# A selective scan in four engines: one state of four scanned in PSUM, its inputs spread by matmuls, its sums kept channels first

## The chip, the cores and the metric

One core of a Trainium2 chip runs the whole program. The metric is device time in microseconds for one execution. A core has five engines with an instruction stream each: TensorE (PE in the profile, with PEld for its weight loads), VectorE (DVE), ScalarE (ACT), GpSimd (POOL) and SyncE (SP). In this program every DMA is issued by SP, in one order. PSUM is the small memory that PE writes; here it is eight tiles of 128 partitions by 512 float32 numbers. POOL has no operand in PSUM in either kernel.

## The reference, cut to what matters

Four images of 64 x 64 tokens and 96 channels go through two state-space layers and then two attention and feed-forward layers (the last two are not touched). Both state-space layers have this core: an input projection and a 3 x 3 convolution give u; u is read in four directions k (rows, columns, and both backwards); for each direction and channel d, sixteen states n are run along the tokens:

```python
xs = [u, u_transposed, u_reversed, u_transposed_reversed]
delta = softplus(dts + bias)
def step(h, inputs):                     # over all tokens, one after the other
    dA = exp(delta[..., None] * A)       # A: one number per channel and state
    h = h * dA + (delta * u)[..., None] * B[:, :, None, :]
    y = einsum('bkdn,bkn->bkd', h, C)    # sum over the 16 states
    return h, y
ys = ys + D * u
y = ys[0] + reversed(ys[2]) + transposed(ys[1]) + transposed(reversed(ys[3]))
y = layer_norm(y) * silu(z)              # z: the other half of the input projection
out = y @ out_proj.T
```

B and C depend on token and state, not on the channel. Layer 0 has 4 images of 4096 tokens and 192 channels. Layer 1 works on the 64 x 33 frequencies of a Fourier transform, so 2112 tokens, with 384 channels, and comes back by an inverse transform.

## The kernel before, in words

Channels lie on partitions, tokens along the free axis. In layer 0 two images share the 128 partitions (64 channels each, NI = 2), so 192 channels make C = 3 chunks; in layer 1 one image has 3 chunks of 128 channels (NI = 1). The work is a list of six phases, two for layer 0 (a pair of images each) and four for layer 1. A phase has four directions, a direction a row of segments: 8 of 512 tokens in layer 0, and 512, 512, 384, 384 and 320 in layer 1. That is 64 segments in layer 0 and 80 in layer 1. A segment has 12 steps: four quads q of four states, times three chunks c. So there are 768 steps in layer 0 (all of 512 tokens) and 960 in layer 1 (384 of 512, 384 of 384 and 192 of 320).

One step takes four states of one chunk:

- ACT makes four tensors of decays, exp(delta * A) (`exp`, L635). Two of them (`ax`) lie in SBUF, made a step ahead; two (`ay`) lie in PSUM.
- For states 0 and 1 (`hx`) the input b = delta * u * B comes from ACT and PE: `make_bx` (L600) multiplies the transposed delta * u, tokens on partitions, by B as a scale per partition, for all three chunks at once, and PE turns it back into a PSUM tile by transposes of 128 x 128 (`transposed`, L630).
- For states 2 and 3 (`hy`) B is loaded by a DMA that repeats its row on all partitions (`broadcast`, L580) and POOL multiplies (`front_b`, L653).
- DVE runs the four recurrences, one `tensor_tensor_scan` each (`scan`, L660), in token order or against it.
- The two pairs are multiplied by C, which comes repeated on all partitions too: `hx` on POOL (L805), `hy` on DVE (L822). The last column of each pair is kept as the state for the next segment (`keep_state`, L673, on POOL or ACT).
- PE adds the products up over the 16 states in a PSUM tile per chunk, by transposes of 128 x 128 that accumulate (`accumulate`, L682): 16 a step at 512 tokens, with the result tokens first. After the last quad ACT takes the sum out (`close_chunk`, L709) and it is stored tokens first, each direction apart.

PSUM's eight tiles are three accumulators (`acc0` to `acc2`), three in a ring for b and `ay` (`ab`), one for preparing the next segment (`pp`) and one for the side work (`ms`).

The order of all engines but SP is written out by hand in the loop over steps, and the engines hold to it. Between the parts of a step stand three slots; a slot takes a piece of the preparation of the next segment (`prepare`: projections to B, C and delta on PE, softplus on ACT in a `burst`, delta * u on DVE, transposes) and, at a rate per phase (`RATES`), a piece of side work. The side work is what the other phases need: input projection and convolution (L176, L274), transposing u (`flip`), z (`gate`), the end of a layer (`gated`) with `out0` or `out1`, the Fourier transforms and the attention layers (`tokens`). `gated` reads the four stored directions back tokens first (`load`), adds D * u (L397, a matmul with a diagonal) and the four directions (L403, transposes) in PSUM, 128 tokens at a time, and goes on with the norm, the gate and the output projection. Side work that PE meets in its order holds up the scan if it has to wait. A head of some 216 us precedes the first scan, and a tail of 390 us follows the last (the end of the last image, run four tasks wide).

Of the kernel before, what the change touches and what calls it, by code (L numbers as in the profile page):

```python
# [29 lines left out]
class Cfg:  # L30
# [5 lines left out]
    def __init__(self, pre, NI, KI, NR, nat, R, parts, rows, segs, eps):  # L36
# [8 lines left out]
        self.eps = eps  # L45


CFG0 = Cfg("l0", 2, 1, HH, 0, 6, [(0, 32), (32, 64)], [8] * 8, [512] * 8, 1e-5)
CFG1 = Cfg("l1", 1, 2, WF, 1, 12, [(0, WF)], [8, 8, 6, 6, 5], [512, 512, 384, 384, 320], 1e-5)
# [74 lines left out]
class Block:  # L124
# [79 lines left out]
    def in_weights(self, sp, g, c, w):  # L204
        cfg = self.cfg
        wi = sp.tile([CH, cfg.KI, 2, cfg.PI], F32, name=f"{cfg.pre}_wi_{g}_{c}", tag=f"wi{w}", bufs=2)
        self.nc.sync.dma_start(out=wi, in_=self.w["inw"][:, :, :, c, :])
        return wi

    def project(self, E, g, io):  # L210
# [8 lines left out]
        def chunk(sp, c, w):  # L219
# [4 lines left out]
            wi = self.in_weights(sp, g, c, w)  # L224
# [127 lines left out]
    def gated(self, E, g, io, out_proj):  # L352
# [5 lines left out]
        yn, yo = io["y"][cfg.nat], io["y"][1 - cfg.nat].rearrange("k (w r) c -> r w k c", r=cfg.NR)  # L358
        u, gz = io["u"][cfg.nat], io["gz"]
        with E.pool(f"{cfg.pre}nm{g}") as sp:  # L360
            wo = sp.tile([P, C, self.w["wo"].shape[2]], F32, name=f"{cfg.pre}_wo_{g}", tag="wo")
            nc.sync.dma_start(out=wo, in_=self.w["wo"])

            def load(b, i, r, n):
                nm = f"{cfg.pre}_{g}_{r}"
                yt = sp.tile([P, 2, 2, C * P], F32, name=f"yt_{nm}", tag=f"yt{b % W}", bufs=2)
                nc.sync.dma_start(
                    out=yt[: n * 64, 0], in_=yn[:, r * 64 : (r + n) * 64, :].rearrange("k t c -> t k c")
                )
                for m in range(n):  # L370
                    nc.sync.dma_start(out=yt[m * 64 : (m + 1) * 64, 1], in_=yo[r + m])
                ut = sp.tile([P, C, P], F32, name=f"ut_{nm}", tag=f"ut{b % W}", bufs=2)
                nc.sync.dma_start(out=ut[:, :, : n * 64], in_=u[:, :, r * 64 : (r + n) * 64])
                return yt, ut

            def worker(w):

                blocks = list(enumerate(cfg.rows))[w::W]
                todo = iter([(b, i, r + i, min(2, n - i)) for b, (r, n) in blocks for i in range(0, n, 2)])
# [4 lines left out]
                for b, (r, nr) in blocks:  # L384
# [5 lines left out]
                    for i in range(0, nr, 2):  # L390
                        m = min(2, nr - i) * 64
                        yt, ut = nxt
                        more = next(todo, None)
                        nxt = load(*more) if more else None
                        ps = E.psum(f"py_{nm}_{i}")[:, : C * P].rearrange("p (c t) -> p c t", c=C)
                        for c in range(C):
                            nc.tensor.matmul(  # L397
                                ps[:, c, :m], self.skip[:, c, :], ut[:, c, :m], start=(c == 0), stop=False
                            )
                        yield  # L400
                        for c in range(C):
                            for k in range(4):
                                nc.tensor.matmul(  # L403
                                    ps[:, c, :m],
                                    yt[:m, k // 2, k % 2, c * P : (c + 1) * P],
                                    self.ident[:m, :m],
                                    start=False,
                                    stop=(c == C - 1 and k == 3),
                                    is_transpose=True,
                                )  # L410
                            if c < C - 1:
                                yield
# [67 lines left out]
def scans(tc, ctx, phases, ident):  # L480
# [239 lines left out]
    with tc.manual_schedule(engines=IN_ORDER):  # L720
# [42 lines left out]
        for i, st in enumerate(steps):  # L763
# [26 lines left out]
            if nxt:  # L790
                nxt.ay = {}
                front_x(nxt)
# [704 lines left out]
```

## Time and profile before

| | |
|---|---|
| median of 3 runs | 11720.34 us (11690.25 to 11727.8) |
| profiled execution, its span | 11704.4 us, 16 us under that median |
| instructions in the trace | 164864 |
| busy share of the span: PE, PEld, DVE, ACT, POOL | 79%, 57%, 90%, 78%, 76% |
| mean granted TensorE clock | 0.880 |
| DMA | 1270879 packets, 1469.07 MB, engines 45.5% busy |

In the rows below, a row names line, engine, operation, what it writes and reads, shape, count, and then the summed time and the mean of one. PE's records overlap, so a busy PE is not a full one: for PE the time from one start to the next is what counts, and it is read from long runs of equal records without a gap. A float32 matmul shows as two records (two passes over its columns); a float32 transpose shows as one. The stages of the kernel are, in microseconds from the span's start: head 0 to 216, the two phases of layer 0 to 2767 and 5353, the four of layer 1 to 6823, 8270, 9791 and 11309, then the tail.

### The profile page before, as it was taken

Reading aid. Unit: us, or ns where it says so; the run is one execution under the profiler, and the core shown is the slowest. Engines: PE = TensorE matmul, PEld = TensorE weight load, DVE = VectorE, ACT = ScalarE, POOL = GpSimd, SP = SyncE. Lnnn points to the kernel's source line nnn. Section 1 sums busy time; section 2 is a strip of 40 time slices with the busy share of each in tenths; the row PEclk is TensorE's granted clock in tenths of the full one; section 3 lists DMA queues with packets and bytes.
Section 4 is the critical chain, followed back from the end, with each engine's and each line's share of the span. In section 5 each row is a group of like instructions: output and inputs, shape, how many; then the busy total and the mean of one; then the engine's idle time right before and its main releaser. Section 6 shows DMA issues by size and latency. Waiting matters only on the chain. (4 is left out here: it accounts for less than half of the span.)

```text
span 11704.4 us, 164864 instructions
## 1 busy us (share of the span) xinstructions
PE 9301.7 (79%) x54800; PEld 6722.3 (57%) x54800; DVE 10549.4 (90%) x10183; ACT 9089.0 (78%) x18533; POOL 8931.5 (76%) x7075
## 2 busy tenths in 40 slices
PE   6678888787888878877888888888778877788765
PEld 3455555555666556555665565565556655565554
DVE  6899999999999998999888989988999999899974
ACT  3778888898888888887767878877787787777753
POOL 2889999887887897897768878877767767677640
PEclk8789999988988998998889989988879988898887
DMA  5454454555555445445544353454225432443242
GB/s 145 120 142 119 126 127 115 141 155 158 153 153 129 124 124 141 120 127 162 153 129 124 114 147 120 142 150 119 88 79 158 122 96 92 124 137 106 83 117 42
DMA packets 1270879, 1469.07 MB, mean 126 GB/s; under 512 B 496071, under 2 KB 1033871, under 8 KB 1260679
## 3 DMA queue, kind: packets, MB, share of 16 engines
q1 hardware_dynamic: 1270023, 1458.53, 45.5%
q8 instruction: 430, 7.05, 0.3%
q14 instruction: 426, 3.49, 0.1%
HBM read 1221.74 MB, written 236.50 MB: 125 GB/s over the span
## 5 line engine op out<-in xcount | busy, mean ns | idle before, releaser
L653 POOL TENSOR_TENSOR hy_l<-du_l,bc_l 128x512 f32<-128x512 f32 (+2 forms) x3456 | 3957.3, 1166 | 1934.8 <-DVE hcy_l L822 960.1
L805 POOL TENSOR_TENSOR hcx_l<-hx_l,bc_l 128x1024 f32<-128x1024 f32 (+2 forms) x1617 | 3525.5, 2180 | 239.1 <-DVE hx_l L660 197.9
L600 ACT ACTIVATE bx_l<-dut_l,bt_l 128x192 f32<-128x192 f32 (+2 forms) x6272 | 2793.7, 498 | 0.0
L682 PE MATMUL acc_l<-ident,hcx_l 128*128 128x128 f32 (+1 forms) x12006 | 1876.0, 305 | 392.6 <-POOL hcx_l L805 388.4
L635 ACT ACTIVATE ax_l<-delta_l,l_alog 128x512 f32<-128x512 f32 (+2 forms) x3456 | 2139.1, 667 | 0.0
L682 PE MATMUL acc_l<-ident,hcy_l 128*128 128x128 f32 (+1 forms) x12000 | 1841.9, 302 | 302.4 <-DVE hcy_l L822 299.0
L682 PEld LDWEIGHTS acc_l<-ident,hcy_l 128*128 128x128 f32 (+1 forms) x12000 | 1551.5, 155 | 859.2 <-DVE hcy_l L822 475.7
L682 PEld LDWEIGHTS acc_l<-ident,hcx_l 128*128 128x128 f32 (+1 forms) x12006 | 1526.4, 156 | 861.5 <-POOL hcx_l L805 665.9
L822 DVE TENSOR_TENSOR hcy_l<-hy_l,bc_l 128x1024 f32<-128x1024 f32 (+2 forms) x1616 | 1951.1, 1207 | 43.6
L660 DVE TENSOR_TENSOR_SCAN hx_l<-ax_l,state_l,b_l 128x512 f32<-128x512 f32 (+2 forms) x1650 | 1787.4, 1124 | 212.7 <-PE b_l L630 136.9
L660 DVE TENSOR_TENSOR_SCAN hy_l<-b_l,state_l,hy_l 128x512 f32<-128x512 f32 (+2 forms) x1649 | 1782.9, 1118 | 89.3 <-ACT b_l L635 81.4
L635 ACT ACTIVATE b_l<-delta_l,l_alog 128x512 f32<-128x512 f32 (+2 forms) x1913 | 1196.6, 628 | 627.6 <-DVE hx_l L660 599.0
L630 PE MATMUL b_l<-ident,bx_l 128*128 128x128 f32 (+1 forms) x6724 | 1169.6, 302 | 363.0 <-DVE hy_l L660 203.5
L635 ACT ACTIVATE ab_l<-delta_l,l_alog 128x512 f32<-128x512 f32 x1321 | 907.1, 689 | 547.5 <-DVE hx_l L660 496.4
L630 PEld LDWEIGHTS b_l<-ident,bx_l 128*128 128x128 f32 (+1 forms) x6724 | 827.1, 152 | 861.3 <-DVE hy_l L660 337.1
L660 DVE TENSOR_TENSOR_SCAN hy_l<-ab_l,state_l,hy_l 128x512 f32<-128x512 f32 x961 | 1172.1, 1257 | 60.8 <-POOL hy_l L653 31.9
L660 DVE TENSOR_TENSOR_SCAN hx_l<-ax_l,state_l,ab_l 128x512 f32<-128x512 f32 x962 | 1176.5, 1263 | 49.3 <-PE ab_l L630 27.3
L630 PE MATMUL ab_l<-ident,bx_l 128*128 128x128 f32 x5288 | 889.1, 305 | 383.2 <-DVE hy_l L660 206.3
L673 POOL COPY state_l<-hx_l 128x2 f32<-128x2 f32 x1344 | 1141.9, 850 | 0.0
L630 PEld LDWEIGHTS ab_l<-ident,bx_l 128*128 128x128 f32 x5288 | 652.0, 154 | 715.6 <-DVE hy_l L660 326.6
L274 PE MATMUL pc_l<-pad_l,l_dg 128*128 128x512 f32 (+2 forms) x1656 | 787.9, 564 | 56.0 <-ACT uh_l L252 46.6
L176 PE MATMUL pi_l<-xi_l,l_wi 96*128 96x384 f32 (+6 forms) x912 | 458.6, 619 | 180.0 <-ACT zh_l L342 60.4
(225 smaller groups left out, 11821.3 us busy)
## 6 DMA issues: line engine op xcount, KB each, us to landing
bc_l<-l_xd_l SPq DMA_DIRECT2D x1536, 256.0 KB
bc_l<-l_xd_l SPq DMA_DIRECT2D x384, 512.0 KB
bc_l<-l_xd_l SPq DMA_DIRECT2D x384, 384.0 KB
us_l<-l_u SPq DMA_DIRECT2D x96, 768.0 KB
l_y<-y_l SPq DMA_DIRECT2D x288, 256.0 KB
bc_l<-l_xd_l SPq DMA_DIRECT2D x192, 320.0 KB
yt_l<-l_y SPq DMA_DIRECT2D x264, 192.0 KB
yt_l<-l_y SPq DMA_DIRECT2D x128, 384.0 KB
```

What stands on the lines that cost most here:

```text
L176: self.nc.tensor.matmul(out[i * cfg.PI : (i + 1) * cfg.PI, :n], wi[:, ki, half, :], xin[:, max(i, ki), :n], start=(ki == 0), stop=(ki == c ...
L274: nc.tensor.matmul(pc[:, : n * 64].rearrange("p (r w) -> p r w", w=64), diag[:, t, :], pad[:, r - p0 + dy : r - p0 + dy + n, dx : dx + 64] ...
L600: nc.scalar.activation(t[:n, b, :, ch], z.dut[:n, b, :, ch], AF.Copy, scale=z.bt[:n, b, m : m + 1])
L630: nc.tensor.transpose(pb[:, t : t + n], st.z.bx[st.q, j][:n, b, st.c], ident[:n, :n])
L635: nc.scalar.activation(out, z.delta[:, st.c, : z.S], AF.Exp, scale=z.blk.A[:, st.c, z.k, n : n + 1])
L653: nc.gpsimd.tensor_tensor(st.hy[:, j, :S], st.z.du[:, st.c, :S], st.z.b[st.q][:, j, :S], ALU.mult)
L660: nc.vector.tensor_tensor_scan(h[:, j, : z.S][:, ::step], a[:, : z.S][:, ::step], b[:, : z.S][:, ::step], 0.0 if z.first else z.state[st.c ...
L673: copy(z.state[st.c][:, n0 : n0 + 2].rearrange("p (j o) -> p j o", o=1), h[:, :, e : e + 1])
L682: nc.tensor.matmul(z.acc[st.c][:n, b, :], hc[:, j, t : t + n], ident, start=(n0 + j == 0 and b == 0), stop=(n0 + j == NST - 1 and b == 0), ...
L805: nc.gpsimd.tensor_tensor(hcx[:, :, :S], hx[:, :, :S], z.c[q][0][:, :, :S], ALU.mult)
L822: nc.vector.tensor_tensor(hcy[:, :, :S], st.hy[:, :, :S], z.c[q][1][:, :, :S], ALU.mult)
```

## The change

Per step, the four states are now treated in this way:

- B-scaled identities in place of B-scaled inputs. ACT multiplies the identity by B as a scale per partition (`make_diagonals`, L606 of the new kernel), 128 x 128 for each block of tokens, image of the pair, and made state. PE multiplies the transposed delta * u by them (`spread_b`, L639), which gives b with channels first. This is done for `made` states: 2 of 4 in layer 0 and 3 of 4 in layer 1. In layer 0 each image of the pair has its own B, so each is a matmul with 64 output partitions. POOL's `front_b` (L665) makes the other 2 or 1.
- One state (`kept` = 1) is scanned in place in its PSUM tile (L676); DVE multiplies it there by C (`multiply_kept`, L694) and ACT saves its last column. The other three lie in one SBUF tile, and POOL multiplies them by C in one instruction (`multiply`, L705), a step later than their scans, and saves their last columns.
- The sum over states is a matmul with the identity as weights over all tokens of the segment (`add`, L713), one per state, with channels first; its result is stored channels first. To a backward direction the forward one of the same kind is added in that sum, and D * u to the first (`fetch_more`, L737).
- `gated` reads two arrays, channels first, in place of four; one lies transposed, and is loaded in runs of 16 or 17 tokens (`load_crossed`, L380). It adds them by two identity matmuls per chunk and up to 512 tokens.
- C is loaded for four states at a time, B for two or one, at the first and second step of a quad. Some buffers of side work lose their second copy. The `ab` ring stays at three tiles.

The order of a step changes with it. Before: scan 0, scan 1, POOL's product, scan 2, scan 3, sums of the first pair, DVE's product, POOL's inputs, sums of the second pair. Now: scan 0, DVE's product of it, POOL's product of the step before, POOL's inputs for the next, the sum of the kept state, scan 1, scan 2, the three sums of the step before, scan 3, with the spreading matmuls of the next step after scans 1, 2 and 3.

```diff
-CFG0 = Cfg("l0", 2, 1, HH, 0, 6, [(0, 32), (32, 64)], [8] * 8, [512] * 8, 1e-5)
-CFG1 = Cfg("l1", 1, 2, WF, 1, 12, [(0, WF)], [8, 8, 6, 6, 5], [512, 512, 384, 384, 320], 1e-5)
+CFG0 = Cfg("l0", 2, 1, HH, 0, 6, [(0, 32), (32, 64)], [8] * 8, [512] * 8, 1e-5, 2, 1)
+CFG1 = Cfg("l1", 1, 2, WF, 1, 12, [(0, WF)], [8, 8, 6, 6, 5], [512, 512, 384, 384, 320], 1e-5, 3, 1)
...
-                    nc.scalar.activation(
-                        t[:n, b, :, ch], z.dut[:n, b, :, ch], AF.Copy, scale=z.bt[:n, b, m : m + 1]
-                    )
+                    nc.scalar.activation(
+                        t[:n, b, i, j, :n], ident[:n, :n], AF.Copy, scale=z.bt[:n, b, m : m + 1]
+                    )
...
-            nc.tensor.transpose(pb[:, t : t + n], st.z.bx[st.q, j][:n, b, st.c], ident[:n, :n])
+            for i in range(z.cfg.NI):
+                ch = slice(i * PI, (i + 1) * PI)
+                nc.tensor.matmul(
+                    pb[ch, t : t + n], z.dut[:n, b, st.c, ch], z.dg[st.q][:n, b, i, j, :n], start=True, stop=True
+                )
...
+            nc.vector.tensor_tensor(hk[:, : z.S], st.px[j][:, : z.S], z.c[st.q][:, j, : z.S], ALU.mult)
...
+        nc.gpsimd.tensor_tensor(st.hc[:, :, :S], st.h[:, :, :S], z.c[st.q][:, kept:, :S], ALU.mult)
...
-                nc.tensor.matmul(
-                    z.acc[st.c][:n, b, :],
-                    hc[:, j, t : t + n],
-                    ident,
-                    start=(n0 + j == 0 and b == 0),
-                    stop=(n0 + j == NST - 1 and b == 0),
-                    is_transpose=True,
-                )
+    def add(st, w, v, first=False, final=False):
+        nc.tensor.matmul(st.z.acc[st.c][:, : st.z.S], w, v[:, : st.z.S], start=first, stop=final)
...
+            scan(st, 0)
+            for j in range(made, 3):
+                front_y(st, j)
             if nxt:
-                nxt.ay = {}
                 front_x(nxt)
+            multiply_kept(st)
+            front_y(st, 3)
+            if closing:
+                close_chunk(closing)
+            closing = None
             long = burst()
-            scan(st, hx, 1, st.ax[:, 1], st.px[1], 4 * q + 1)
+            if before:
+                multiply(before)
+            if nxt:
+                front_b(nxt)
+            add_kept(st)
...
             slot(None)
+            scan(st, 1)
...
+                spread_b(nxt, 0)
             more.take(skip=long)
-            scan(st, st.hy, 0, st.ay[0], st.hy[:, 0], 4 * q + 2)
+            scan(st, 2)
+            if before:
+                add_rest(before)
+                closing = before if before.q == NQ - 1 else None
+            slot(None, hold=long)
             if nxt:
-                nxt.px.append(transposed(nxt, 1))
-            slot(None, hold=long)
-            scan(st, st.hy, 1, st.ay[1], st.hy[:, 1], 4 * q + 3)
+                spread_b(nxt, 1)
+            scan(st, 3)
+            if nxt:
+                for j in range(2, nxt.z.cfg.made):
+                    spread_b(nxt, j)
```

## The prediction

> **What bounds the kernel now.** I read four views: the page's engine shares, busy time by stage, the timeline of a steady stretch, and long gapless runs on PE for the price of a matmul. First the page:
>
> ```profile
> PE 9301.7 (79%) x54800; PEld 6722.3 (57%) x54800; DVE 10549.4 (90%) x10183; ACT 9089.0 (78%) x18533; POOL 8931.5 (76%) x7075
> ...
> L653 POOL TENSOR_TENSOR hy_l<-du_l,bc_l 128x512 f32<-128x512 f32 (+2 forms) x3456 | 3957.3, 1166 | 1934.8 <-DVE hcy_l L822 960.1
> L805 POOL TENSOR_TENSOR hcx_l<-hx_l,bc_l 128x1024 f32<-128x1024 f32 (+2 forms) x1617 | 3525.5, 2180 | 239.1 <-DVE hx_l L660 197.9
> ```
>
> DVE is busiest. The six scan stages (stretch; then PE, PEld, DVE, ACT, POOL busy, the clock granted to PE, DMA share, GB/s) say the same everywhere:
>
> ```profile
> 216.00:2767.00 2551.00, 1966.03 (x10846) 1355.87 (x10844) 2419.42 (x1992) 2167.24 (x4485) 2264.40 (x1643) 0.89 0.50 130
> 2767.00:5353.00 2586.00, 2099.21 (x12844) 1592.02 (x12843) 2436.35 (x2041) 2179.46 (x4537) 2213.66 (x1598) 0.90 0.53 137
> 5353.00:6823.00 1470.00, 1251.74 (x7299) 917.10 (x7298) 1306.77 (x1310) 1105.06 (x2120) 1142.68 (x968) 0.88 0.48 138
> 6823.00:8270.00 1447.00, 1236.57 (x7383) 882.46 (x7382) 1295.60 (x1303) 1124.74 (x2186) 1146.69 (x975) 0.90 0.46 131
> 8270.00:9791.00 1521.00, 1200.79 (x7235) 873.21 (x7233) 1425.94 (x1576) 1176.99 (x2429) 1079.85 (x932) 0.86 0.36 107
> 9791.00:11309.00 1518.00, 1185.08 (x7259) 869.74 (x7258) 1411.42 (x1558) 1155.70 (x2376) 1076.84 (x932) 0.87 0.36 105
> ```
>
> DVE is busy 10,295 of 11,093 us in the scans, 92.8%. One step of layer 0 on DVE, from one `hx` pair to the next, has no gap over 0.1 us and takes 6.14 us:
>
> ```profile
> 3008.64 2.45 DVE L660 TENSOR_TENSOR_SCAN hx_l<-ax_l,state_l,b_l 128x512 f32<-128x512 f32 x2
> ...
> 3011.01 2.43 DVE L660 TENSOR_TENSOR_SCAN hy_l<-b_l,state_l,hy_l 128x512 f32<-128x512 f32 x2
> ...
> 3013.48 1.22 DVE L822 TENSOR_TENSOR hcy_l<-hy_l,bc_l 128x1024 f32<-128x1024 f32 x1
> ...
> 3014.78 2.45 DVE L660 TENSOR_TENSOR_SCAN hx_l<-ax_l,state_l,b_l 128x512 f32<-128x512 f32 x2
> ```
>
> So half of L822 would be the gain, if nothing else takes DVE's place. For PE, busy time overstates, so I price it by pitch, the time from start to start:
>
> ```profile
> 3021.16 1.04 PE L682 MATMUL acc_l<-ident,hcy_l 128*128 128x128 f32 x8
> ```
>
> ```profile
> 79.95 14.00 PE L274 MATMUL pc_l<-pad_l,l_dg 128*128 128x512 f32 x32
> 93.89 1.72 PE L176 MATMUL pi_l<-xi_l,l_wi 96*64 96x448 f32 x4
> ```
>
> ```profile
> 11417.24 1.61 PE L397 MATMUL py_l<-ut_l,l_skip 128*128 128x128 f32 x12
> 11418.68 1.58 PE L403 MATMUL py_l<-ident,yt_l 128*128 128x128 f32 x13
> ```
>
> ```profile
> 11494.68 20.16 PE L1026 MATMUL piv<-ih,at 128*64 128x64 f32 x320 [1.51 <-DMA at<-att]
> ```
>
> A transpose of 128 columns costs (1.04 - 0.27 for the last one's latency) / 7 = 0.11 us. A float32 matmul is two records: at 512 columns each is 13.94 / 32 = 0.435, so 0.87 a matmul; at 128 columns each is 1.44 / 12 = 0.12, so 0.24. L1026 alternates two halves of 64 outputs, as the new L639 does in layer 0: 20.16 / 320 = 0.063 a record, at 64 columns.
>
> PE's work now is 24 transposes a step at 512 tokens (8 of L630, 16 of L682) and 18 at 384 and 320. 1152 x 24 x 0.11 + 576 x 18 x 0.11 = 4,182 us. The other PE records in the scan stages, at columns x 0.85 ns (0.435 / 512): L527 and L537 673, convolution L274 576, L176 299, L568 171, L403 and L397 222, the rest about 710; 2,650. Together 6,830 of 11,093 us: PE has 38% free.
>
> **The change, part by part.**
>
> *Sums (L713).* A step at 512 tokens now has four identity matmuls, 4 x 0.87 = 3.48 us, for 16 transposes, 1.76. At 384 and 320 tokens 2.61 and 2.18. The added earlier direction or D * u (nine in four segments of 12 steps, so 0.19 a step) is 0.16, 0.12, 0.10. The pass of 512 columns is certain to 0.43 to 0.46 (the same L274 in a stretch of lower clock).
>
> The Trainium skill ("TensorE: Matmul & The Clock Gate", Terms) calls transpose mode four times faster for FP32, a rule against this change. The rows above make it twice: 0.44 for four transposes, 0.87 for one matmul over the same columns. By the rule the four sums would be 7.0 us a step and the kernel some 19 ms, an estimate from that page; the rows decide.
>
> *Spreading (L639), layer 0.* 2 states x 4 blocks x 2 halves = 16 matmuls, 32 records, for 8 transposes (0.88). No row has 128 columns into halves. Low end: the halves overlap fully at the pitch of a transpose, 0.055 a record, 1.76 us a step. High end: none overlap, L397's 0.12, 3.84. I take L1026's 0.063, the same alternation: 2.02. Layer 1: 12 matmuls of full width at 512 tokens, 2.88; 9 at 384 and 320, 2.16 (down to 0.11 a record, 10% less).
>
> *PE in sum.* Layer 0: (2.02 + 3.48 + 0.16) x 768 = 4,347. Layer 1: 6.52 x 384 + 4.89 x 384 + 4.44 x 192 = 5,234. 9,581 in all, 5,399 more than now. Of the other 2,650 some 150 goes: the end of a layer takes six matmuls per block in place of L397 and L403 (222 to about 147), and L176's halves in layer 0 overlap, which I had not counted. PE has 9,581 + 2,500 = 12,080 us to do in scans that take 11,093 now.
>
> *DVE.* Four scans stay (1.26 at 512). The product falls from 1.31 to 0.67 (L421 has one PSUM and one SBUF operand: 666 ns). Writing a scan into PSUM has no row: 0 as for PSUM inputs, within 0.1 us either way, beside PE. That frees about 960 us, on an engine no longer the bound: nothing in the sum.
>
> *POOL.* Layer 0: 2 x 1.27 + 2.36 x 1.5 + 0.19 = 6.27 a step, layer 1 one input less; under PE's 5.66 plus about 1.45 of other work. L673's save has a minimum of 175 ns and a median of 1,177 beside L822. The Trainium skill ("SBUF — State Buffer", Who interferes with whom) says that a DVE instruction with two SBUF inputs contends with a POOL one that reads SBUF, and one with a single SBUF input does not; then the new product in PSUM leaves POOL alone. It is worth about 1 us a step to POOL and nothing to the sum.
>
> *ACT.* Four exponentials as before; layer 0's 16 multiplies per quad shrink from 192 to 128 elements (442 ns; the save of two elements is 190), layer 1's are 12 of 128 for 8 of 384 (603). Equal or less; hidden beside PE.
>
> *The order and the new waits.* The three sums wait for POOL's product of the step before; behind them on PE are a slot and the second spreading matmul, for which scan 1 of the next step waits. POOL starts that product right after scan 3 and needs 3.6 us; PE reaches the sums after scan 2, 3 us or more into the step, so this costs little. The next spreading matmul needs a ring tile that scan 1 or 2 frees. While PE is behind, DVE waits for it at scan 1.
>
> *DMA and SP.* B and C take 4 issues a quad for 6 in layer 0, 2 for 3 in layer 1; fewer stores; three added loads a segment, issued two steps ahead. All covered. New are 14 loads of the transposed array inside the scans, three issues each of 8,192 runs of 64 bytes. The nearest row is L310, 8,192 runs of 128 bytes; the issue behind it on SP held for 7 us:
>
> ```profile
> 281.00 0.40 SPq L310 DMA_DIRECT2D l_u<-ut_l  x1
> 281.44 7.08 SPq L323 DMA_DIRECT2D fl_l<-l_u  x1
> ```
>
> So 21 us each for loads of B and C queued behind, which have two steps (13 us) of cover, and for PE at the first use. 0 to 14 x 21 = 294; I take 4 us each, 56.
>
> *The sum.* PE never fully packs: the bound engine's share lies between DVE's 92.8% of now and 100%; I take the middle, 96.4%. 12,080 / 0.964 = 12,531; head and tail 216 + 390 as now; 56: 13,193. The profiled execution (span 11,704) is 16 us under the median of 11,720, less than I can resolve. I say 13,190, 12.5% slower.
>
> **Rivals.**
>
> *PE absorbs it (faster).* For it: 38% of PE is free, and the clock could rise from 0.89. Then POOL bounds layer 0 at 6.27 + 0.18 for its side work: 768 x 6.45 = 4,954 for 5,137. Layer 1 follows DVE, less 960 steps x 0.53: at today's ratio of stage to busy time (5,956 / 5,440) 558 us. 11,704 - 183 - 558 = 10,963. Against it: PE's work would have to fit 10,357 us, so the 512-column record would have to cost about 0.3, not 0.435; from 0.37 on there is no gain. No row goes below 0.43.
>
> *The halves do not overlap.* 3.84 for 2.02 a step: + 1,398 / 0.964 = 1,450: 14,640. For it: no row at 128 columns. Against: L1026.
>
> *The short-run loads hold SP.* Every load costs its 21 us, and waits on POOL's product bring PE down to 92.8%: 12,080 / 0.928 + 606 + 294 = 13,917. For it: the 7 us above; against: only 14 loads, and PE queues other work.
>
> **How the numbers follow.** The main case, PE bound and well packed (12,370 to 13,600), 0.68; PE absorbs it 0.05; no overlap 0.10; loads and waits 0.17. The main case's low end: 200 less in layer 0's spreading, 120 less in layer 1's, no waits: 12,080 - 320 + 606 = 12,366. The range, 12,430 to 14,150, leaves out the faster case, most of no-overlap, and slivers. A measurement tells about 0.3% from no change; only the first rival falls under that: faster 0.05, same 0.01, slower 0.94.
>
> **What would show it.** Right: PE's idle share near nil, a clock near 1.0, gaps on DVE at scan 1 released by PE's L639 and on the sums; L713 pitch 0.435; L639 near 0.063 in layer 0; DVE under 80%. Wrong: DVE or POOL without gaps while PE waits; an L713 record under 0.37; or idle time released by the DMAs of L380.

## The result, and the profile after

The changed kernel takes 14641.13 us, median of 4 runs (14632.26 to 14653.08), where the kernel before took 11708.32 in the runs beside it: 1.25 times as long, 95% interval 1.2477 to 1.2523. I had said 13,190, and 14,150 at most. The direction was right, and so was the engine; the loss is 1,450 us larger than I said.

The page of the changed kernel, its engine shares and three of its costliest groups (busy time, mean ns, then the idle time in front and what ended it):

```profile
PE 13614.1 (93%) x73472; PEld 8121.7 (55%) x73472; DVE 10207.3 (70%) x10183; ACT 8743.1 (60%) x19704; POOL 8933.7 (61%) x5960
...
L705 POOL TENSOR_TENSOR hc_l<-h_l,bc_l 128x1536 f32<-128x1536 f32 (+2 forms) x1728 | 5579.7, 3229 | 4901.9 <-DVE h_l L676 2850.1
L713 PE MATMUL acc_l<-hc_l,ident 128*128 128x512 f32 (+2 forms) x10368 | 4502.4, 571 | 26.9 <-POOL hc_l L705 26.9
...
L676 DVE TENSOR_TENSOR_SCAN h_l<-ax_l,state_l,b_l 128x384 f32<-128x384 f32 (+2 forms) x1365 | 1420.5, 1065 | 1357.3 <-PE b_l L639 1263.9
```

PE has taken DVE's place. DVE, which had next to no gaps, now waits in front of its scans until PE has spread b (L639). POOL stands idle for 4,902 us in front of its product, so POOL is not the limit. The same by stage (stretch; PE, PEld, DVE, ACT, POOL busy; granted clock; DMA share; GB/s):

```profile
214.00:3241.00 3027.00, 2878.44 (x17117) 1461.84 (x17118) 2202.82 (x1993) 2043.46 (x4529) 2417.93 (x1599) 0.99 0.46 116
3241.00:6533.00 3292.00, 3120.28 (x18659) 1654.34 (x18660) 2262.34 (x2041) 2073.21 (x4579) 2405.72 (x1559) 0.97 0.46 109
6533.00:8492.00 1959.00, 1914.65 (x9369) 1262.96 (x9368) 1236.73 (x1309) 1090.66 (x2417) 1017.76 (x713) 0.98 0.36 93
8492.00:10421.00 1929.00, 1816.68 (x8865) 1192.39 (x8865) 1331.71 (x1401) 1122.71 (x2559) 1030.00 (x709) 0.97 0.30 85
10421.00:12398.00 1977.00, 1791.40 (x9012) 1192.46 (x9011) 1501.30 (x1559) 1139.07 (x2667) 1030.71 (x676) 0.96 0.28 76
12398.00:14268.00 1870.00, 1741.34 (x8753) 1155.15 (x8752) 1422.20 (x1480) 1095.74 (x2554) 1018.59 (x676) 0.97 0.25 75
```

Every stage is longer; head and tail are near what they were (214 and 372 us, 216 and 395 before). Two things here will matter later: the clock is not 1.0, and DVE is busy up to 265 us longer in the last two stages than in the third, where in the kernel before it was up to 119.

The timeline of a step of layer 0 shows what PE does:

```profile
4499.75 1.45 PE L713 MATMUL acc_l<-hc_l,ident 128*128 128x512 f32 x3
...
4501.14 1.09 PE L639 MATMUL b_l<-dg_l,dut_l 128*64 128x128 f32 x16
...
4502.16 1.12 PE L541 MATMUL pp_l<-xs_l,l_dtw 76*128 76x512 f32 x2
4502.35 1.28 DVE L676 TENSOR_TENSOR_SCAN h_l<-ax_l,state_l,b_l 128x512 f32<-128x512 f32 x1 [1.16 <-PE b_l L639]
...
4503.12 1.02 PE L713 MATMUL acc_l<-k_l,ident 128*128 128x512 f32 x2
...
4504.07 1.09 PE L639 MATMUL b_l<-dg_l,dut_l 128*64 128x128 f32 x16
```

Sixteen records of L639 take 1.09 us, less 0.27 for the last one's own length 0.82, so 0.055 from start to start: a pair of halves costs what one full record costs. They do overlap, at the low end of what I allowed. But look at the seams. Three records of L713 should take 3 x 0.429 = 1.29 from their start to the next group's; they take 1.39. The sixteen should take 0.87; the next group starts 1.02 after them. The two of L541 take 0.96 for 0.86. Each visit to the half-width matmuls costs about 0.35 us (0.10 in front, 0.15 behind, 0.10 in the next group) that none of the records in its middle shows, and in layer 0 there are two a step.

**Where the time on PE went.** I took every PE record in the scans from the trace and split the time to the next start. Streaming is the pitch that its shape has in the middle of a run at full clock; what goes beyond it is "half clock" if the record starts while the granted clock is one half (the trace has only full and half), "shape" if the number of active rows or columns changes within two records of it (up to 0.2 us a record, so that small waits near a change are in it), and "wait" if it is larger.

| us in the scans | before | predicted for after | after |
|---|---|---|---|
| streaming | 6,777 | 12,080 | 11,735 |
| shape changes | 372 | none | 1,073 |
| half clock | 1,068 | none | 326 |
| waits | 2,672 | 451 | 934 |
| small rest | 204 | none | -15 |
| the scans | 11,093 | 12,531 | 14,052 |

The borders between the rows are a choice: other rules as plausible move some 300 us between half clock and waits in the kernel before, and 100 to 150 us between the rows of the changed one. The streaming that I priced is right to 3%. The 1,521 us that are missing lie beside it. Shape changes grew by 701 us. Layer 0's visits would be 0.35 x 2 x 768 = 538 of them if each cost what the clear ones do; the run without them, below, puts them at 483. The rest, some 200, is about 0.35 x 3 x 192 for the last block of layer 1's segments of 320 tokens, which has 64 tokens.

PE's longest waits in the changed kernel (total, times, longest):

```profile
PE acc_l L713 <- DVE k_l L694: 239.5, 113, 8.2
PE acc_l L713 <- DVE hk_l L694: 201.2, 79, 7.0
PE b_l L639 <- DVE h_l L676: 84.2, 85, 2.8
PE py_l L403 <- DMA yt_l<-l_y: 76.1, 4, 23.6
```

The largest, 441 us, is for DVE's product of the kept state, a wait that I had not named.

### The profile page after: what moved, and what is told of

Read it like the earlier page. It is cut to its first block, busy times and chain, and to the rows that moved or that the text cites. A ratio compares the mean times of both kernels' runs of the same rounds, so it can differ in the third digit from the quotient of the medians.

```text
span 14639.8 us, 200838 instructions
## 1 busy us (share of the span) xinstructions
PE 13614.1 (93%) x73472; PEld 8121.7 (55%) x73472; DVE 10207.3 (70%) x10183; ACT 8743.1 (60%) x19704; POOL 8933.7 (61%) x5960
## 5 line engine op out<-in xcount | busy, mean ns | idle before, releaser
L705 POOL TENSOR_TENSOR hc_l<-h_l,bc_l 128x1536 f32<-128x1536 f32 (+2 forms) x1728 | 5579.7, 3229 | 4901.9 <-DVE h_l L676 2850.1
L713 PE MATMUL acc_l<-hc_l,ident 128*128 128x512 f32 (+2 forms) x10368 | 4502.4, 571 | 26.9 <-POOL hc_l L705 26.9
L665 POOL TENSOR_TENSOR h_l<-du_l,bc_l 128x512 f32<-128x512 f32 (+2 forms) x2496 | 3005.1, 1217 | 205.1 <-DMA bc_l<-l_xd_l 66.7
L639 PEld LDWEIGHTS b_l<-dg_l,dut_l 128*64 128x64 f32 (+2 forms) x24480 | 2181.4, 162 | 1084.2 <-issue 424.2
L713 PEld LDWEIGHTS acc_l<-hc_l,ident 128*128 128x128 f32 x10368 | 1880.0, 195 | 1592.7 <-issue 1293.0
L639 PE MATMUL b_l<-dg_l,dut_l 128*64 128x128 f32 (+2 forms) x24480 | 2539.2, 284 | 85.9 <-DVE h_l L676 84.2
L606 ACT ACTIVATE dg_l<-ident,bt_l 128x128 f32<-128x128 f32 (+1 forms) x7360 | 2352.8, 389 | 125.0 <-PE ab_l L639 63.0
L676 DVE TENSOR_TENSOR_SCAN h_l<-ax_l,state_l,b_l 128x384 f32<-128x384 f32 (+2 forms) x1365 | 1420.5, 1065 | 1357.3 <-PE b_l L639 1263.9
L639 PEld LDWEIGHTS ab_l<-dg_l,dut_l 128*64 128x64 f32 (+1 forms) x19680 | 1729.6, 164 | 841.6 <-issue 435.3
L639 PE MATMUL ab_l<-dg_l,dut_l 128*64 128x128 f32 (+1 forms) x19680 | 1933.7, 280 | 72.3 <-DVE h_l L676 69.3
L676 DVE TENSOR_TENSOR_SCAN h_l<-ax_l,state_l,ab_l 128x512 f32<-128x512 f32 x843 | 1046.7, 1270 | 843.1 <-PE ab_l L639 782.9
L676 DVE TENSOR_TENSOR_SCAN h_l<-b_l,state_l,h_l 128x512 f32<-128x512 f32 (+2 forms) x1292 | 1461.9, 1153 | 149.1 <-ACT b_l L645 143.6
L676 DVE TENSOR_TENSOR_SCAN b_l<-ax_l,state_l,b_l 128x512 f32<-128x512 f32 (+2 forms) x885 | 991.8, 1121 | 449.7 <-PE b_l L639 442.0
L713 PE MATMUL acc_l<-k_l,ident 128*128 128x512 f32 (+2 forms) x2036 | 973.2, 560 | 241.6 <-DVE k_l L694 239.5
L676 DVE TENSOR_TENSOR_SCAN h_l<-ab_l,state_l,h_l 128x512 f32<-128x512 f32 x820 | 1014.9, 1261 | 61.8 <-ACT ab_l L645 58.3
L713 PE MATMUL acc_l<-hk_l,ident 128*128 128x512 f32 x1420 | 786.9, 637 | 202.1 <-DVE hk_l L694 201.2
L676 DVE TENSOR_TENSOR_SCAN ab_l<-ax_l,state_l,ab_l 128x512 f32<-128x512 f32 x555 | 709.2, 1278 | 219.4 <-PE ab_l L639 214.8
```

The costliest lines, as they stand in the source:

```text
L606: nc.scalar.activation(t[:n, b, i, j, :n], ident[:n, :n], AF.Copy, scale=z.bt[:n, b, m : m + 1])
L639: nc.tensor.matmul(pb[ch, t : t + n], z.dut[:n, b, st.c, ch], z.dg[st.q][:n, b, i, j, :n], start=True, stop=True)
L665: nc.gpsimd.tensor_tensor(st.h[:, j - kept, :S], z.du[:, st.c, :S], z.b[st.q][:, j - made, :S], ALU.mult)
L676: nc.vector.tensor_tensor_scan(h[:, ::step], a[:, ::step], b[:, ::step], 0.0 if z.first else z.state[st.c][:, n : n + 1], ALU.mult, ALU.add,)
L705: nc.gpsimd.tensor_tensor(st.hc[:, :, :S], st.h[:, :, :S], z.c[st.q][:, kept:, :S], ALU.mult)
L713: nc.tensor.matmul(st.z.acc[st.c][:, : st.z.S], w, v[:, : st.z.S], start=first, stop=final)
```

## The experiments

"Theory 1" in the expectations below is what the trace suggests: PE sets the time, its halves overlap, and what I missed lies in the seams and the waits. A time given without a range is one run; the seven runs of the kernel before in one set spread by at most 0.5%.

**Halves apart.** The measured 14,641 is what my rival "the halves do not overlap" gave, within a microsecond, so that had to be told apart first.

```diff
-        for b, (t, n) in enumerate(z.blocks):
-            for i in range(z.cfg.NI):
+        for i in range(z.cfg.NI):
+            for b, (t, n) in enumerate(z.blocks):
```

> Layer 0's spreading matmuls in another order: all blocks of the first 64 channels, then all blocks of the second 64. The changed kernel's 14,641 us is just what the rival with halves that do not overlap gave. Theory 1, the halves of a pair do overlap in the changed kernel (two records in 0.109 us): apart they cannot, 32 records a step go from 0.055 to 0.11 us each, +1.76 us x 768 steps = +1,350 us, about 15,990. Rival, the halves do not overlap as it is: the order costs nothing, 14,640 within 60.

Measured: 15249.66 us, 609 more. The timeline of this run:

```profile
4499.27 1.58 PE L639 MATMUL b_l<-dg_l,dut_l 128*64 128x128 f32 x16
4500.78 1.13 PE L713 MATMUL acc_l<-k_l,ident 128*128 128x512 f32 x2
```

The order matters, so in the changed kernel the halves overlap and the rival falls; the agreement of the two numbers was chance. My size was off: records of the same half follow each other in (1.58 - 0.27) / 15 = 0.087 us, not 0.11.

**Full width in layer 0.** The same streaming time without a visit to half-width matmuls:

```diff
-            for i in range(z.cfg.NI):
-                ch = slice(i * PI, (i + 1) * PI)
+            for i in range(1):
+                ch = slice(0, P)
```

> Layer 0's spreading with one matmul of full width a block, the first image's B for both images, in place of two of half width: the values of B for the second image are left out, so this is not the reference's result. Theory 1, PE bounds the kernel and each visit to half-width matmuls costs 0.39 us of entering and leaving (0.093 before it, 0.05 in it, 0.15 and 0.1 after it) beside the records themselves: 16 full records x 0.112 = 1.79 us replace 32 x 0.055 = 1.75, and two visits a step go, 2 x 0.39 x 768 = 600 us: about 14,080. Rival A, the halves do not overlap: 16 records of 0.112 fewer a step, -1,380 us, 13,260. Rival B, what is lost around these groups is waiting for other engines: 14,640 within 100.

Measured: 14396.97 us, 244 less. The seams are gone in its timeline:

```profile
4500.69 0.81 PE L275 MATMUL pc_l<-pad_l,l_dg 128*128 128x384 f32 x2
4501.33 1.05 PE L639 MATMUL b_l<-dg_l,dut_l 128*128 128x128 f32 x8
4502.22 2.74 PE L713 MATMUL acc_l<-hc_l,ident 128*128 128x512 f32 x6
4504.80 0.81 PE L275 MATMUL pc_l<-pad_l,l_dg 128*128 128x384 f32 x2
```

From start to start 0.64 for two of 0.322, 0.89 for eight of 0.111, 2.58 for six of 0.43: nothing left over. By the split above, shape changes fall from 1,073 to 590 us, 0.31 for each of 1,536 visits, and all of PE's own work (the table without its waits) by 339. I had expected 560. And of the 339 only 244 reached the time, because waits grew by 94. That the price of a seam is not waiting is shown by this run: the groups stand in the same places, behind the same semaphores. But it also has half as many matmuls. Layer 1 of the changed kernel tells the two apart. There six records of L639 stand between two groups of L713, at 384 tokens all of full width, at 320 tokens the last two with 64 rows and 64 columns:

```profile
6797.15 0.83 PE L639 MATMUL b_l<-dg_l,dut_l 128*128 128x128 f32 x6
6797.81 1.46 PE L713 MATMUL acc_l<-hc_l,ident 128*128 128x384 f32 x4
...
7020.59 0.97 PE L639 MATMUL b_l<-dg_l,dut_l 128*128 128x128 f32 x6
7021.49 1.34 PE L713 MATMUL acc_l<-hc_l,ident 128*128 128x320 f32 x4
```

From start to start the first six take 0.66 us, the other six 0.90, though they have less to stream; and the first record behind takes 0.325 at 384 tokens (0.323 in the middle of its group), but 0.373 at 320 (0.269). So it is the active shape, not the number of matmuls. The Trainium skill has a sentence that fits ("TensorEngine Tiling (Array Packing)", Tiling Modes, Key Properties): to change the tiling mode, not only the tile, drains TensorE. I had not weighed that sentence. No price stands beside it, and no row here shows a drain as such; the rows give 0.35 us a visit.

**Two sums less.**

```diff
-        for j in range(many):
+        for j in range(many - 1, many):
             add(st, ident, st.hc[:, j], final=(st.q == NQ - 1 and j == many - 1))
```

> Two of the four matmuls of a step that sum over states are left out (states 1 and 2 of each four are missing from the sums). Theory 1, PE's stream sets the time: 1152 steps x 2 x 2 x 0.429 or 0.322 or 0.269 a record (768 + 384 steps at 512 tokens, 384 at 384, 192 at 320) = 1,977 + 495 + 207 = 2,680 us go, 11,960, or up to 12,300 where other engines begin to take PE's place. Rival, what PE waits for sets the time: under 300 us go, 14,340 or more. A floor by my first rival of before, where POOL and DVE bound: 10,963.

Measured: 13031.33 us, 1,610 less, in the middle between the two. Streaming fell by 2,677 as worked out; but waits grew from 934 to 1,779 us and half clock from 326 to 630. So PE bounds the changed kernel, but not alone: for each us taken from it 0.6 goes (1,610 of 2,677).

**One state less on PE in layer 1.** `CFG1` with made = 2.

> Layer 1 spreads b of two states on PE, not three; POOL multiplies the third by the broadcast B. Theory 1, PE sets the time: a third spreading group goes, 0.90 us x 384 + 0.67 x 384 + 0.96 x 192 (there with the visit to a half-size block) = 786 us: 13,850. POOL's added product, 1.25, 0.94 and 0.79 us a step, 993 us in sum, on 4,096 of busy time in layer 1's 7,735 stays under PE. Rival, POOL's product of the step before is what the sums wait for in layer 1: the longer POOL step gives most of it back, 14,300 or more.

Measured: 14315.78 us, 325 less, 0.4 of what PE saved. The number is the rival's, its reason is not: PE's wait for POOL's product (L705) stays at 28 us, 27 before. It is the wait for DVE's product (L694) that grew, from 441 to 597 us.

Something beside PE's load keeps the kernel slow. The next runs take the change apart: each part alone, put on the kernel before, or left out.

**The kept state alone.** The kernel before, with state 0 scanned and multiplied in PSUM, and with the changed kernel's order of a step; transposes for b and for the sums as before.

```diff
+        st.h = sp.tile([P, 3, SM], F32, name=f"h_{st.nm}", tag="h", bufs=3)
...
+        h = st.px[j][:, :S] if j < 1 else st.h[:, j - 1, :S]
...
+        nc.vector.tensor_tensor(st.hk[:, : z.S], st.px[0][:, : z.S], z.c[st.q][:, 0, : z.S], ALU.mult)
...
+        nc.gpsimd.tensor_tensor(st.h[:, :, :S], st.h[:, :, :S], z.c[st.q][:, 1:, :S], ALU.mult)
```

> The kernel before with one part of the change alone: one of four states scanned in PSUM and multiplied by DVE, POOL multiplies the other three by C in place, in the changed kernel's order of steps; b of two states still comes from transposes, the sums are still transposes into sums with tokens first. Theory 1, the loss is PE's added matmuls: with PE back at before's work (streaming 6,777 us of 11,093) DVE's halved product shows, POOL bounds layer 0 at 768 x 6.45 and DVE layer 1, the 10,963 us of my first rival, up to 11,300. Rival, the new order of waits (the kept product on DVE ahead of PE's first sum, the sums of the step before) costs by itself: from the run with two sums less (13,031 us at 9,058 of streaming, 0.6 us of time for each us taken from PE) 13,031 - 0.6 x 2,281 = 11,660, no gain over before.

Measured: 12325.29 us (12309.23 to 12329.44), 1.053 of before, interval 1.0513 to 1.0548. Not a gain but a loss of 622 us, with PE's streaming as before (6,778), and past the rival's number too. Its engine shares, and the two stages of layer 0:

```profile
PE 9202.4 (75%) x54800; PEld 6900.7 (56%) x54800; DVE 10224.5 (83%) x10183; ACT 9023.7 (73%) x18688; POOL 9960.2 (81%) x6920
```

```profile
215.00:2799.00 2584.00, 1909.58 (x10840) 1393.26 (x10840) 2218.09 (x1992) 2138.49 (x4528) 2412.27 (x1599) 0.89 0.51 129
2799.00:5477.00 2678.00, 2068.86 (x12852) 1612.27 (x12851) 2272.81 (x2042) 2155.00 (x4573) 2404.60 (x1561) 0.90 0.54 132
```

POOL is busy 93% and 90% there. The floor under my first rival, 10,963, is not reached: without any of PE's new load this order gives 12,325. In layer 1 POOL has one product a step more here than in the changed kernel, which makes three states on PE; the run with POOL relieved, below, leaves that product out.

**The spreading alone.** The kernel before with `make_bx` and `transposed` replaced by `make_diagonals` and `spread_b` for two states.

> The kernel before with b of two states by B-scaled identity matmuls in both layers, and nothing else of the change. PE's streaming grows by 1,336 us in layer 0 and 1,573 in layer 1 less 1,344 of transposes, 1,565, and by 1,536 + 384 visits to half-size matmuls at 0.35 us, 672. Theory 1, PE works in DVE's shadow as long as it stays under some 85% of the scans (6,777 + 372 + 2,240 = 9,390 of 11,093): 11,700 to 12,200. Rival, each us on PE counts at 0.6 because DVE and PE wait for each other in every step: 11,720 + 0.6 x 2,240 = 13,060.

Measured: 11846.16 us, 143 more, as theory 1 has it. In the old order PE's own work grows by 985 us (8,421 to 9,406, that is from 76% to 84% of the scans) and costs 143.

**The sums without the spreading.** The changed kernel with `transposed` for two states in both layers; for its memory `hk` and `y` have one buffer, not two.

> The changed kernel with b of two states by transposes as before, in both layers: sums with channels first and the state kept in PSUM stay. Against the run with two states made in layer 1 (14,316 us; streaming 11,009, shape changes 981) PE loses 1,565 us of streaming and some 670 of visits. Theory 1, PE sets the time: 2,240 less, 12,080; with the 0.6 of the runs so far, 12,970. Rival, sums by full matmuls are not what costs and the time falls to before's: under 11,900.

Measured: 13314.59 us, above every number I gave; 1,001 less than with the spreading of two states (14,316).

**The sums undone.** Transposes into sums with tokens first. With them go the stores tokens first, `gated` with its four arrays, and POOL's product in place, all as in the run with the kept state alone; the kept state and the spreading of two or three states stay.

```diff
-        nc.tensor.matmul(st.z.acc[st.c][:, : st.z.S], w, v[:, : st.z.S], start=first, stop=final)
+                z.acc[st.c][:n, b, :],
+                v[:, t : t + n],
+                ident,
+                start=(n0 == 0 and b == 0),
+                stop=(n0 == NST - 1 and b == 0),
+                is_transpose=True,
```

> The changed kernel with the sums undone: four groups of transposes a step into sums with tokens first, as before; b of two or three states by matmuls and the state kept in PSUM stay. PE's streaming falls by 5,620 and grows by 2,730, 11,735 to about 8,850. Theory 1, the sums are the largest part of the loss, and without them POOL bounds layer 0 as in the run with the kept state alone (5,262 us) and DVE layer 1, whose POOL has a product less: 606 + 5,262 + 5,900 to 6,450: 11,770 to 12,320. Rival, each us of PE counts 0.6 whatever it is: 14,641 - 0.6 x 2,885 = 12,910.

Measured: 12873.42 us, 1,768 less than the changed kernel; the rival's 12,910 was near. Together these give the loss by parts (the kernel before was at 11,703 to 11,730 beside them):

| step | us | added |
|---|---|---|
| before | 11,703 | |
| kept state and the new order | 12,325 | 622 |
| sums channels first | 13,315 | 989 |
| b of two states by matmuls | 14,316 | 1,001 |
| a third in layer 1 | 14,641 | 325 |

Each row of the table is a run less the one before it. The run of the third row also has one buffer fewer for `hk` and for `y`, so its 989 and the 1,001 after it are not the price of the named part alone. The sums and the spreading cost far more on top of each other. The spreading of two states is 143 on the kernel before; of two and three states it is 548 on the kept state (12,873 less 12,325) and 1,326 with the sums there too. The sums are 989 without the spreading and 1,768 with it. PE's own work, as a share of the scans, is 76% before, 84% and 85% in the runs without one of the two, 91% with two states made in layer 1 and 93% in the changed kernel.

**The sum of the kept state later.** PE's 441 us of waiting for L694 might go if PE came to it later.

```diff
-            add_kept(st)
             if (q, c) in ((NQ - 2, 1), (NQ - 2, 2), (NQ - 1, 0)):
...
                 closing = before if before.q == NQ - 1 else None
+            add_kept(st)
             slot(None, hold=long)
```

> The changed kernel with PE's sum of the kept state moved behind the sums of the step before: PE then meets DVE's product 2 to 3 us later in the step. PE waits 441 us for that product (L694) in the changed kernel. Theory 1, this wait is on PE's path: 200 to 440 us go, 14,200 to 14,440. Rival, PE's waits only move to the next thing DVE is late with: 14,640 within 60.

Measured: 15064.74 us, 424 more; both expectations miss. PE's waits in this run:

```profile
PE b_l L639 <- DVE h_l L676: 307.7, 250, 9.2
PE ab_l L639 <- DVE h_l L676: 279.7, 218, 6.1
```

The wait for L694 is gone, and 587 us of waiting for a tile of the `ab` ring (154 before) take its place: the next spreading needs a tile that scan 1 frees, and PE now comes to it with nothing to do in between. But these two cancel: 441 and 154 are 595. What grew lies in other waits. All of PE's waits in this view go from 1,014 to 1,355 us. The largest new ones are 104 for ACT's save of the kept state's last column (L698, none before) and 102 for DVE's side operations L1253 and L1266 (11 before):

```profile
PE ab_l L639 <- ACT state_l L698: 59.3, 42, 5.1
PE ph L1259 <- DVE x L1253: 52.0, 53, 3.3
PE pfo L1271 <- DVE h L1266: 49.5, 43, 3.0
PE b_l L639 <- ACT state_l L698: 44.6, 37, 2.5
```

Why these grew when PE's sum moved is open.

**POOL relieved.** What costs 622 us in the run with the kept state alone? First POOL:

```diff
-        for j in range(2, 4):
+        for j in range(2, 3):
             nc.gpsimd.tensor_tensor(st.h[:, j - 1, :S], z.du[:, st.c, :S], z.b[st.q][:, j - 2, :S], ALU.mult)
...
-        b = st.px[j][:, :S] if j < 2 else h
+        b = st.px[j][:, :S] if j < 2 else h if j < 3 else z.b[st.q][:, 1, :S]
```

> The run with the kept state alone, and POOL's product of du and B for the last of four states left out: that scan takes the broadcast B itself, so its values are not the reference's. POOL has 1.27 us a step less at 512 tokens, 0.98 and 0.84 at 384 and 320. Theory 1, POOL bounds layer 0 there (busy 6.4 of 6.85 us a step): layer 0 falls to what DVE needs, 6.2 / 0.95 = 6.5, 270 us, and layer 1 by up to 150 as DVE's side operations meet POOL less: 11,900 to 12,060. Rival, the loss is PE and DVE waiting for each other over the kept product (PE waits 1,170 us for it): 12,325 within 60.

Measured: 11985.71 us, 340 less, as theory 1 said:

```profile
214.00:2680.00 2466.00, 1870.30 (x10842) 1373.85 (x10842) 2176.60 (x1993) 2137.41 (x4530) 1956.18 (x1216) 0.91 0.53 135
2680.00:5247.00 2567.00, 2035.77 (x12847) 1604.72 (x12846) 2238.35 (x2040) 2153.06 (x4573) 1946.71 (x1176) 0.90 0.55 138
```

Layer 0 falls from 5,262 to 5,033 us, below the 5,137 of the kernel before. So with the kept state POOL holds layer 0 back, though a microsecond of its work is not one of time: 914 us of it went there, and 229 of time. Layer 1 falls from 6,450 to 6,339; before it was 5,956.

**POOL's product split.** In the last two stages the run with the kept state alone is at 3,422 us, before at 3,039, and POOL is not full there. One timeline of the changed kernel suggests why:

```profile
10556.95 4.07 DVE L1263 TENSOR_SCALAR h<-h,b 128x512 f16<-128x512 f16 x3
10557.17 3.44 POOL L705 TENSOR_TENSOR hc_l<-h_l,bc_l 128x1536 f32<-128x1536 f32 x1 [1.35 <-PE ab_l L639]
```

Three DVE operations of 0.35 us each take 4.07 together: the second one starts 0.02 us behind POOL's product, and ends 0.15 behind its end.

```diff
-        nc.gpsimd.tensor_tensor(st.h[:, :, :S], st.h[:, :, :S], z.c[st.q][:, 1:, :S], ALU.mult)
+        parts = [(0, 3)] if z.cfg.NI == 2 else [(0, 1), (1, 2), (2, 3)]
+        for j0, j1 in parts:
+            nc.gpsimd.tensor_tensor(st.h[:, j0:j1, :S], st.h[:, j0:j1, :S], z.c[st.q][:, 1 + j0 : 1 + j1, :S], ALU.mult)
```

> The run with the kept state alone, and in layer 1 POOL multiplies its three states in three instructions, not one. DVE's side operations there take 1.3 us on average for 0.33 (h<-h,b), up to 3.5, when they start beside POOL's product of 2.9 us: by theory 1 they are held until POOL's instruction ends, and a third of its length holds them a third as long: of about 400 us of such excess 200 go, most of it in the last two stages, 12,080 to 12,200, less some 100 that three instructions cost POOL. Rival, these operations are slow for another reason: 12,325 or more.

Measured: 12157.25 us, 168 less, as expected. All of it lies in the last two stages, 3,240 us for 3,422. The last run does the same split in the changed kernel.

> The changed kernel with POOL's product of three states split into three instructions in layer 1, as in the run that split it beside the kept state alone. There it gave 168 us, as DVE's side operations were held for less long. In the changed kernel PE waits 251 of its 441 us for DVE's kept product (L694) in the last two stages, where these operations lie. Theory 1, that part of PE's waiting comes from DVE being held by POOL, and adds to PE's own work: the mean of h<-h,b falls from 1.27 to about 0.8 us, half of the 251 us goes, 14,500 to 14,560. Rival, PE's own work sets the time and its waits only shift: 14,640 within 40.

Measured: 14379.37 us (14370.26 to 14389.41), 1.2282 of before (1.2254 to 1.231): 262 less than the changed kernel, more than either theory had. The same line in the kernel before, the changed one, and this one (shortest, median and longest in ns):

```profile
L1211 DVE TENSOR_SCALAR h<-h,b x192: 326/344/877, 8346.0 to 11695.7; 128x512 f16<-128x512 f16 x192
```

```profile
L1263 DVE TENSOR_SCALAR h<-h,b x192: 325/347/3582, 10077.7 to 14631.1; 128x512 f16<-128x512 f16 x192
```

```profile
L1267 DVE TENSOR_SCALAR h<-h,b x192: 326/353/1432, 10029.9 to 14378.9; 128x512 f16<-128x512 f16 x192
```

The longest follows what is left of POOL's instruction when DVE's operation starts. In the changed kernel it meets a product of 3.45 us at its start. In the last run the longest, 1.43, stands beside POOL's other product (L665, 1.27 us), and the longest beside one of the three parts (1.3 us) is 1.37. In the kernel before, it met a product of 1.81 us only 1.08 after its start. In the eight longest of each of these kernels DVE ends 0.15 us behind POOL. With the split DVE's busy time in layer 1 falls by 208 us, PE's wait for L694 from 441 to 291 us (160.0 and 130.8 in this run's waits), and half clock from 326 to 209. No run here beats the kernel before.

## Why the prediction was wrong

By its own steps:

- **What bounds, and what will.** Right. DVE was the bound; PE is now, DVE is at 70%, and DVE's gaps end with L639.
- **Sums (L713).** Right: 0.429 us a record at 512 columns (0.435 taken), 5,604 us of streaming for 5,679.
- **Spreading (L639).** Right, at the low end of what I allowed, for the records in the middle of a group: 0.055 a record in layer 0 (0.063 taken), 0.112 in layer 1 (0.12): 3,484 us for 3,901.
- **The other 2,500 of PE.** 2,648. Half of the difference lies in one operation, L405, which reads the crossed array with a stride (below).
- **DVE.** The product is 0.692 us (0.67), the scan into PSUM 1.28 for 1.26: right, and nothing in the sum. But DVE's side operations in layer 1 grew from 662 to 1,046 us, which I had not counted.
- **POOL.** The save of the state falls from a mean of 850 ns (L673) to 207 (L708), about as I read from L673. But that was only half: I looked at DVE holding POOL, not at POOL's product of 3.45 us holding DVE. And I took one SBUF input to be enough to keep DVE clear of POOL; L1263 has one tensor there and was held.
- **The order and the new waits: "little".** Wrong. The order with the kept state costs 622 us alone. In the sum the wait for L694, 441 us, was not named at all.
- **DMA.** The 56 us taken are not there. PE waits 76 us for what `gated` loads, but 66 before (L397), and 183 for all loads, 203 before. For loads of B and C only POOL waits to speak of (66.7 us), and POOL is not the limit.
- **The sum.** This is the step that failed. I divided 12,080 us of streaming by 0.964 because "PE never fully packs", and that share, between DVE's 92.8% and 100%, was to hold everything beside streaming: 451 us. It measured 2,317. PE is indeed kept 93% busy with its own work (13,119 of 14,052), near the low end. But its work is not its streaming: 1,073 us of shape changes, a term that the sum has not, and 326 of half clock, where I had "a clock near 1.0" (0.967). Streaming is 345 less, waits 483 more than taken: -345 + 1,073 + 326 + 483 - 15 = 1,522, the 1,521 that are missing in the scans. Head, tail and loads are 76 less than taken (586 for 662), which leaves the 1,450. Two runs on the changed kernel take parts of it away again: 244 us without layer 0's seams, 262 with POOL's product split. The rest is read from the split of the trace alone; no run here turns off the half clock or the other waits by themselves.

The rivals: "the halves do not overlap" gave the right number for a wrong reason; its extra 1,450 us are the seams, the clock and the waits. "PE absorbs it" was priced from a floor of 10,963 that the kept state alone does not reach by 1,360 us. In layer 0 that is 308: the floor had POOL as the bound there, but busy 97% where it is 90 to 93%. In layer 1 it is 1,052: the floor had DVE's busy time fall from 5,440 to 4,931 us, and DVE as full as before. DVE's product did fall, from 1,034 us to 574, but the side operations, which count as busy while they are held, grew from 662 to 1,082: DVE's busy time is 5,478 us, 85% of the time there. Against the kernel before, the kept state costs 125 of its 622 us in layer 0, which relieving POOL more than takes back (229), and 494 in layer 1. Of these 494 relieving POOL takes 111 and the split 170, and the two may overlap; the rest, 213 at least, stays open. "The short-run loads hold SP" fails in both parts: PE waits no longer for loads than before, and 27 us for POOL's product.

## What to carry to other kernels

Price a group of matmuls from its start to the next group's start, not by the pitch in its middle: where the active shape of the array changes, entering and leaving cost as much as several records. Where two engines wait for each other in every step, a microsecond taken from the bound one is not a microsecond of time: here it was 0.4 to 0.7, and added work cost 143 us while another engine was the bound (two states spread in the old order), 548 in the new order (two and three states), and 1,326 with the sums on PE as well. And before an engine's relief is counted as a floor, try that part alone: the work that it hands over (three states in one POOL instruction) may cost more than it frees; here that part alone lost 622 us.

## What the runs showed of the hardware

- A change between matmuls of 128 and of 64 output columns costs about 0.35 us for a visit of sixteen records (0.10 in front, 0.15 behind, 0.10 in the next group); between full-width groups of different lines and lengths nothing is seen (2.58 us for six records of 0.43).
- Alternating halves take 0.055 us a record, records of the same half 0.087, a full-width record 0.111.
- A DVE operation on float16 (L1263, one tensor in SBUF and a number per partition) that takes 0.35 us lasted up to 3.58 beside a POOL product of 3.45, and up to 1.37 beside one of three parts of it. The Trainium skill ("SBUF — State Buffer", Who interferes with whom) says that one SBUF input keeps a DVE instruction clear of GpSimd only outside the two-port modes, and that in such a mode whichever of the two issues first has the shared ports for its whole instruction and the other one is blocked. These rows agree with the second part, and the split shows that the length of the one instruction sets the price; which mode DVE was in no row shows.
- The mean clock went with PE's load: 0.880 before (PE busy 79%), 0.967 after (93%), 0.948 with the spreading alone (86%), 0.865 with the kept state alone (75%).
- A matmul whose moving operand is read with a stride took twice as long here: the two records of L405 (from `yx`, 17 numbers apart) against those of L403 (from `yt`, in order), both of 512 columns; less the last one's own 1.07 and 0.59 they are 0.90 and 0.43 us apart.

```profile
3310.28 1.02 PE L403 MATMUL py_l<-yt_l,ident 128*128 128x512 f32 x2
...
3313.49 2.00 PE L405 MATMUL py_l<-yx_l,ident 128*128 128x512 f32 x2
```
